# Query rows summed from PSUM, a second key pair in plain products, and a pair's last two products issued inside the next pair

## The chip, the cores and the metric

The kernel runs on one core of a Trainium2 chip. The metric is the device time of one execution in microseconds, from start to end, as the median of several runs. The core has a matrix engine (TensorE, in the profile PE, with its weight loads as PEld), a vector engine (VectorE, DVE), a scalar engine (ScalarE, ACT), GpSimd (POOL), and SyncE (SP), on whose queue this kernel issues its DMAs. TensorE writes only to PSUM, which has eight banks here; one product of 128x512 float32 fills one bank. All other tiles lie in SBUF.

## The reference, cut to what matters

There are 8 batch entries b of 128 rows x 512. Two layers run one after the other; the change concerns the first part of the first one, a gated cross attention with 32 heads of 128.

```python
x = rmsnorm(layernorm(hidden)) * ln_weight          # 8 x 128 x 512
h_q = (x @ w_q.T).reshape(b, 128, 32, 128)
h_k = (ctx @ w_k.T).reshape(b, 128, 32, 128)
h_v = (ctx @ w_v.T).reshape(b, 128, 32, 128)
score = softmax(where(mask, einsum('bqhd,bkhd->bhqk', h_q, h_k) + position_bias, -inf))
attn = einsum('bhqk,bkhd->bqhd', score, h_v)
out = hidden + attn.reshape(b, 128, 4096) @ w_out.T
```

Behind it come a dense layer with 4-bit weights, a second cross attention with a single head, and a dense layer with routed low-rank corrections; each is added to x through a gate tanh(g). All is float32.

## The kernel before, in words

**Products in three parts.** A float32 operand is split into a high part, rounded to the type that TensorE multiplies fast, and a low part, the rest (`split`, L162: the high by ACT at L163, the low by DVE or POOL at L164). A product is then three matmuls per 128 of the inner dimension: high x high, high x low, low x high (`product`, L166, lines 172 to 174).

**Seven products for eight.** Keys, queries and values are made by blocks of 2x2 with Winograd's scheme (`seven`, L219). A pair is two heads (2 x 128 output rows) by 512 inner by 1024 tokens. The left side (the weights) needs seven sums P1 to P7 (`left_parts`, L198), the right side (the transposed rows of all batch entries) seven blocks B11, B21, B22 and T1 to T4. Each of the seven products is six matmuls of 128x512. They are issued in the order P1, P5, P6, P2, P7, P4, P3 and add up in three PSUM banks: c1 takes P1, P6, P7 and P4, c3 takes P5 and P3, c2 takes P2. Between its uses c1 is read by copies of ACT: L251 after P1, L258 after P6, L267 after P7, L273 after P4. Sums on DVE follow (L262 after P2, L268 after P7, L277 after P3). So P7 has to wait for the copy of P6, P4 for the copy of P7, and P3 for the sum at L268. The four results of a pair lie in "kq" slots and go to DRAM (L493).

**The first pair** of keys is made plainly, in eight products of six matmuls, from the weights' rows split as they are and from the blocks B11, B12, B21, B22 of the context (`project_plainly`, L497), with two banks of "mm" and two of "av"; ACT copies them out at L517.

**The right sides.** `context_operands` (L429) splits the context's B blocks first (ACT high; POOL and DVE low), and then forms T1 to T4 on DVE (L451) and splits these. `query_operands` (L455) makes the rows of a pair of batch entries j and j+4 ready: `normed` (statistics and scaling on DVE, L416 to L422, a root on POOL, a scaling on ACT, L423), eight transposes on TensorE into two "av" banks, two copies to SBUF on ACT (L466), and then `right_parts` (L184): four sums on DVE and seven splits, lows on POOL. It is called after pairs 2, 5, 8 and 11 and does all of one j in one go.

**The order.** 32 pairs are made in this order: 14 of keys, 16 of queries, 2 of keys (L801). Pair n+2's weights are loaded and pair n+1's sums are formed while pair n is multiplied. Between them stand the steps of `early` (L715): 26 steps that load later weights, split them (ACT high, POOL low, some DVE) and store them to DRAM, one step after each pair from pair 3 on, save 5, 8 and 11; and `residual` (L531).

**The stages behind.** `unit(u)` (L867) runs 64 times: two output products of an earlier unit (`project_out`, "pso", in "mm" banks, evicted by DVE at L678), steps of the value products (`seven` with 256 columns, c1 in "mm", c3 in "av", c2 in "sc"), `attend` (L647, an "av" bank, read by ACT at L660 and DVE at L661) and `scores` (L596, an "sc" bank). The probabilities go through DRAM to be transposed by blocks (`move_probs`, L627, and L644). The rest of the layers runs at the end in `pipeline`, whose order on TensorE is kept as written.

**Slots, banks and planning.** Tiles with the same tag share a number of slots (`TAGS`) or banks (`BANKS`: 4 "mm", 2 "sc", 2 "av"); a new tile waits until the one that had its slot is read for the last time. When the kernel is built, a planner decides the order of the instructions on each engine with times of its own: of what is ready it takes what stands first in the program. So the program's order is a priority and not the order itself, except in `pipeline`. Each engine then runs its list strictly in order.

## Time and profile before

| | us |
|---|---|
| median of 3 runs | 1005.44 (1001.28 to 1006.37) |
| the profiled execution | 1005.73 |
| its span, first to last instruction | 1004.0 |
| TensorE (PE) busy | 937.9 (93%) |
| weight loads (PEld) busy | 808.1 (80%) |
| VectorE (DVE) busy | 664.1 (66%) |
| ScalarE (ACT) busy | 513.1 (51%) |
| GpSimd (POOL) busy | 495.5 (49%) |
| mean granted clock of TensorE | 0.983 |

Roughly, the projections of keys and queries fill the first 350 us, the units of attention the stretch to 860 us, and the later layers the rest. Busy time of TensorE overlaps from matmul to matmul: a matmul of 128x512 is listed with about 0.39 us, and the next one starts 0.23 us after it. So what a matmul costs in a row of them is the distance of the starts. "Waits" are idle times of an engine, put down to what ended them. A tile's name stands without its number (c_k is any of the banks c1, c2, c3 of a key pair).

### The profile page before, as it was taken

What the parts mean: (1) busy time and instruction counts of PE and PEld (TensorE: products, weight loads), DVE (VectorE), ACT (ScalarE), POOL (GpSimd) and SP (SyncE); (2) the same over time, 40 slices, a digit from 0 to 9 for tenths busy, and PEclk for the clock granted to TensorE, in tenths of its full rate; (3) what the DMA queues carried; (4) which work ended last, traced back from release to release, by engine and by line L of the source; (5) the groups of instructions that cost most, each with busy time, mean ns of one, the idle gap of its engine ahead of it and who ended that gap; (6) DMA issues with size and microseconds to landing.
All of it is one profiled execution on the core that took longest, in us unless ns stands there. A gap on an engine that the chain in (4) does not pass through costs nothing. (4 is left out here: it accounts for less than half of the span.)

```text
span 1004.0 us, 16700 instructions
## 1 busy us (share of the span) xinstructions
PE 937.9 (93%) x5438; PEld 808.1 (80%) x5438; DVE 664.1 (66%) x1335; ACT 513.1 (51%) x1444; POOL 495.5 (49%) x542
## 2 busy tenths in 40 slices
PE   6799999998999998999999999899999999899998
PEld 4568776776888798889989879788898898778897
DVE  7886576899666424666766576466765667645586
ACT  5566565754544544544434435244452453575762
POOL 4755355444000464683946638456486762462431
PEclk9899999999999999999999999899999999999999
DMA  8356567996545558765666766547565566613001
GB/s 284 110 168 207 161 192 247 321 313 201 182 149 162 156 160 246 226 186 170 184 184 157 200 165 176 182 128 205 169 176 182 166 180 199 220 43 129 1 22 64
DMA packets 125270, 175.01 MB, mean 174 GB/s; under 512 B 17406, under 2 KB 55294, under 8 KB 124030
## 3 DMA queue, kind: packets, MB, share of 16 engines
q1 hardware_dynamic: 125182, 173.94, 57.3%
q8 instruction: 43, 0.70, 0.3%
q14 instruction: 45, 0.37, 0.1%
HBM read 109.85 MB, written 64.03 MB: 173 GB/s over the span
## 5 line engine op out<-in xcount | busy, mean ns | idle before, releaser
L615 ACT ACTIVATE s<-s,nm 128x128 f32<-128x128 f32 x256 | 99.8, 391 | 166.8 <-DVE nm L608 98.1
L591 POOL TENSOR_TENSOR s<-mneg,bias 128x512 f32<-128x512 f32 x64 | 82.9, 1297 | 97.9 <-DMA through<-s 86.1
L644 DVE STREAM_TRANSPOSE pT<-moved 128x512 f32<-128x512 f32 x64 | 45.4, 710 | 98.5 <-DMA moved<-through 98.2
L164 POOL TENSOR_TENSOR wvP<-raw_wv,wvP 128x512 fp32r<-128x512 f32 x45 | 57.5, 1293 | 105.4 <-ACT wvP L163 105.4
L172 PE MATMUL pso<-wo_h,a 128*128 128x512 f32 x256 | 108.2, 423 | 0.4 <-ACT a L660 0.4
L174 PE MATMUL pso<-wo_h,a 128*128 128x512 f32 x256 | 102.6, 403 | 2.0 <-DVE a L661 2.0
L173 PE MATMUL pso<-wo_l,a 128*128 128x512 f32 x256 | 102.4, 400 | 0.0
L678 DVE SCALAR_TENSOR_TENSOR x<-pso,tg,x 128x512 f32<-128x512 f32 x128 | 93.3, 735 | 7.9 <-PE pso L174 7.8
L622 POOL TENSOR_TENSOR s<-s,rs 128x512 f32<-128x512 f32 x64 | 66.5, 1039 | 60.8 <-ACT wo_h L163 18.9
L172 PE MATMUL c_v<-wvP,cxT 128*128 128x256 f32 x288 | 83.1, 289 | 1.5 <-ACT v L267 0.7
L173 PE MATMUL c_v<-wvP,cxT 128*128 128x256 f32 x288 | 81.9, 284 | 0.0
L174 PE MATMUL c_v<-wvP,cxT 128*128 128x256 f32 x288 | 81.6, 284 | 0.0
L659 PE MATMUL av<-pT,v 128*128 128x128 f32 x512 | 69.9, 279 | 12.4 <-DVE a L661 11.5
L659 PEld LDWEIGHTS av<-pT,v 128*128 128x128 f32 x512 | 64.7, 193 | 17.7 <-issue 9.7
L603 PE MATMUL sc<-k,q 128*128 128x128 f32 x512 | 71.6, 280 | 4.3 <-DVE s L604 3.6
L603 PEld LDWEIGHTS sc<-k,q 128*128 128x128 f32 x512 | 66.6, 195 | 7.7 <-DVE s L604 4.5
L172 PE MATMUL c_v<-wvP,cxB 128*128 128x256 f32 x216 | 62.4, 289 | 5.0 <-DVE s L604 2.1
L173 PE MATMUL c_v<-wvP,cxB 128*128 128x256 f32 x216 | 61.4, 284 | 0.0
L174 PE MATMUL c_v<-wvP,cxB 128*128 128x256 f32 x216 | 60.9, 284 | 0.0
L172 PE MATMUL c_k<-cxT,wkP 128*128 128x512 f32 x120 | 49.3, 411 | 12.0 <-ACT keys L267 7.8
L172 PEld LDWEIGHTS c_v<-wvP,cxT 128*128 128x128 f32 x288 | 55.5, 193 | 5.2 <-ACT v L267 2.0
L174 PEld LDWEIGHTS pso<-wo_h,a 128*128 128x128 f32 x256 | 48.6, 190 | 13.4 <-DVE a L661 2.8
(270 smaller groups left out, 2811.6 us busy)
## 6 DMA issues: line engine op xcount, KB each, us to landing
keys<-keys SPq DMA_DIRECT2D x64, 256.0 KB, 3.5
queries<-queries SPq DMA_DIRECT2D x64, 256.0 KB, 2.9
q<-queries SPq DMA_DIRECT2D x64, 256.0 KB, 4.0
k<-keys SPq DMA_DIRECT2D x64, 256.0 KB, 4.7
through<-s SPq DMA_DIRECT2D x64, 256.0 KB, 2.6
moved<-through SPq DMA_DIRECT2D x256, 64.0 KB, 2.7
raw_wk<-in_wk_dram SPq DMA_DIRECT2D x32, 256.0 KB, 3.3
raw_wq<-in_wq_dram SPq DMA_DIRECT2D x32, 256.0 KB, 3.9
```

Of the source, the lines that this page charges most:

```text
L164: mark("low", (low_engine or nc.vector).tensor_tensor(low, src, wide(high), ALU.subtract))
L172: nc.tensor.matmul(out, lhsT=lh, rhs=rh, start=first, stop=False, **more)
L173: nc.tensor.matmul(out, lhsT=lh, rhs=rl, start=False, stop=False, **more)
L174: nc.tensor.matmul(out, lhsT=ll, rhs=rh, start=False, stop=last, **more)
L591: nc.gpsimd.tensor_tensor(s, mneg[:, half], bias.unsqueeze(2).to_broadcast([P, NQ, HALF, Q32]), ALU.add)
L603: nc.tensor.matmul(ps[:, j, :], lhsT=q[:, cols], rhs=k[:, cols], start=True, stop=True)
L615: e = nc.scalar.activation(one, one, AF.Exp, bias=nm[:, j : j + 1], accum_out=sm[:, j : j + 1])
L622: nc.gpsimd.tensor_tensor(s, s, rs.unsqueeze(1).unsqueeze(3).to_broadcast([P, NQ, HALF, Q32]), ALU.mult)
L644: nc.vector.transpose(by_block(t), probs[u])
L659: nc.tensor.matmul(av[:, b, :], lhsT=v[:, cols], rhs=pT[:, b, :], start=True, stop=True)
L678: "x", nc.vector.scalar_tensor_tensor(xs[b], ps, factor, xs[b], ALU.mult, ALU.add, **out)
```

## The change

The banks become 3 "mm", 2 "sc" and 3 "av". Pairs 0 and 1 of the keys are both made plainly, and the T blocks of the context are formed after the first of them. The seven sums of pair 2 have the lows of P1, P2 and P4 on POOL, as those of the pairs behind it had and have.

`query_operands` no longer copies the transposed rows to SBUF. The transposed blocks b11, b21 (one bank) and b12, b22 (the other) are read where they are: ACT copies b11 and takes the highs of B11, B21 and B22 from PSUM, DVE takes their lows and forms T1, T2 and T4 with one input in PSUM each; POOL forms T3 from SBUF. It comes in three pieces per j, one after each of the pairs 2 to 13: the first as above, the second T3 and the splits of T1 and T2, the third the splits of T3 and T4.

`project` now returns its steps, and the loop takes them so: P1 of the pair, P4 of the pair before, P5, P3 of the pair before, P6, P2, P7. The steps of `early` begin after pair 13, two after each pair.

```diff
--- before.py
+++ after.py
@@ -30,7 +30,7 @@
 RANK = 16
 MASKED = 1e30
 
-BANKS = {"mm": 4, "sc": 2, "av": 2}
+BANKS = {"mm": 3, "sc": 2, "av": 3}
 TAGS = {
     "page": 14, "v": 15, "wo": 8, "raw": 6, "kq": 6, "s": 3, "moved": 2, "pT": 2, "bias": 2,
     "pr": 4, "sel": 4,
@@ -181,20 +181,6 @@
     HK = NDC // 2
     N = HK * P
 
-    def right_parts(b11, b12, b21, b22, put):
-
-        put("B11", b11)
-        nc.vector.tensor_tensor(b11, b12, b11, ALU.subtract)
-        put("T1", b11)
-        nc.vector.tensor_tensor(b11, b22, b11, ALU.subtract)
-        put("T2", b11)
-        put("B21", b21)
-        nc.vector.tensor_tensor(b12, b22, b12, ALU.subtract)
-        put("T3", b12)
-        nc.vector.tensor_tensor(b21, b21, b11, ALU.subtract)
-        put("T4", b21)
-        put("B22", b22)
-
     def left_parts(a11, a12, a21, a22, more, engine, put):
 
         put("P1", a11)
@@ -454,6 +440,8 @@
 
     def query_operands():
 
+
+
         ops = right_pages("xq")
         for j in range(HALF):
             rows = [normed(j), normed(j + HALF)]
@@ -462,17 +450,31 @@
                 tp = ptile([P, NDC, P], "av", f"tpx_{j}_{half}")
                 for dc in range(NDC):
                     nc.tensor.transpose(tp[:, dc, :], rows[half][:, bass.ts(dc, P)], ident)
-                t = slot([P, NDC, P], "wo", f"xt_{j}_{half}")
-                nc.scalar.copy(t, tp)
-                blocks.append(t)
-            e, f = blocks
+                blocks += [tp[:, :HK], tp[:, HK:]]
+            b11, b21, b12, b22 = blocks
             cols = bass.ts(j, P)
 
-            def put(n, src):
+            def put(n, src, low=nc.gpsimd):
                 o = ops[n]
-                split(o[:, 0, :, cols], o[:, 1, :, cols], src, nc.gpsimd)
-
-            right_parts(e[:, :HK], f[:, :HK], e[:, HK:], f[:, HK:], put)
+                split(o[:, 0, :, cols], o[:, 1, :, cols], src, low)
+
+            def block(name):
+                return slot([P, HK, P], "wo", f"x{name}_{j}")
+
+            first, t1, t2, t3, t4 = (block(n) for n in ("B11", "T1", "T2", "T3", "T4"))
+            nc.scalar.copy(first, b11)
+            for n, src in (("B11", b11), ("B21", b21), ("B22", b22)):
+                put(n, src, nc.vector)
+            nc.vector.tensor_tensor(t1, b12, first, ALU.subtract)
+            nc.vector.tensor_tensor(t2, b22, t1, ALU.subtract)
+            nc.vector.tensor_tensor(t4, b21, t2, ALU.subtract)
+            yield
+            nc.gpsimd.tensor_tensor(t3, t2, first, ALU.subtract)
+            put("T1", t1)
+            put("T2", t2)
+            yield
+            put("T3", t3)
+            put("T4", t4)
             yield ops
 
     stored = {
@@ -492,7 +494,7 @@
         def done(i, half, t):
             nc.sync.dma_start(out=stored[kind, p][:, 2 * i + half], in_=t)
 
-        run(seven(f"{kind[0]}{p}", left, right, kept, done))
+        return seven(f"{kind[0]}{p}", left, right, kept, done)
 
     def project_plainly(kind, p, left, right):
 
@@ -797,44 +799,60 @@
         yield
 
 
+    BY_POOL = ("P1", "P2", "P4")
     BEFORE = NP - 2
     order = [("keys", p) for p in range(BEFORE)] + [("queries", p) for p in range(NP)]
     order += [("keys", p) for p in range(BEFORE, NP)]
-    first = []
-    for h in range(2):
-        high, low = (wide_row("v", f"wk_{n}{h}", F32R) for n in "hl")
-        split(high, low, raws.pop(f"wk_{h}"))
-        first.append((high, low))
+    def whole_pair(p):
+
+        both = []
+        for h in range(2 * p, 2 * p + 2):
+            high, low = (wide_row("v", f"wk_{n}{h}", F32R) for n in "hl")
+            split(high, low, raws.pop(f"wk_{h}"))
+            both.append((high, low))
+        return both
+
+    PLAIN = 2
+    left = whole_pair(0)
     making = context_operands()
     of_context = next(making)
-    project_plainly("keys", 0, first, of_context)
-    next(making)
     of_rows = query_operands()
     extra = early()
-    left = pair_parts("wk", 1)
+    before = iter(())
     for n, (kind, p) in enumerate(order):
-        if n == 0:
-            load_pair("wk", 2)
-            continue
         if n + 2 < len(order):
             k, q = order[n + 2]
             load_pair("w" + k[0], q)
+        if n < PLAIN:
+            project_plainly(kind, p, left, of_context)
+            left = whole_pair(p + 1) if p + 1 < PLAIN else pair_parts("wk", p + 1, BY_POOL)
+            if n == 0:
+                next(making)
+            continue
         following = None
         if n + 1 < len(order):
             k, q = order[n + 1]
-            following = pair_parts("w" + k[0], q, ("P1", "P2", "P4") if n < BEFORE else ())
-        project(kind, p, left, of_context if kind == "keys" else right)
+            following = pair_parts("w" + k[0], q, BY_POOL if n < BEFORE else ())
+        steps = project(kind, p, left, of_context if kind == "keys" else right)
         left = following
+
+        for _ in range(2):
+            next(steps)
+            next(before, None)
+        for _ in range(3):
+            next(steps)
+        before = steps
         if n == 3:
             prep_mask()
-        if n in (2, 5, 8, 11):
+        if n < BEFORE:
             right = next(of_rows)
         if n in (14, 16, 18, 20):
             residual((n - 14) // 2)
-        if n > 2 and n not in (5, 8, 11):
+        if n >= BEFORE - 1:
             next(extra, None)
-    for _ in extra:
-        pass
+            next(extra, None)
+    run(before)
+    run(extra)
     load_quad(0)
     run(quad_parts(0))
     for u in range(2):
```

## The prediction

> **What bounds the kernel now.** I read the stretches first, to see where TensorE is not full. Their columns are the stretch, then busy us and instructions of PE, PEld, DVE, ACT and POOL, then the granted clock, DMA share and GB/s.

> ```profile
> core 0: us, PE busy (x) PEld busy (x) DVE busy (x) ACT busy (x) POOL busy (x), PEclk, DMA share, GB/s
> 0.00:50.00 50.00, 33.37 (x117) 23.67 (x118) 39.13 (x79) 26.26 (x55) 28.73 (x46) 0.93 0.62 198
> 50.00:150.00 100.00, 93.53 (x399) 74.24 (x400) 71.83 (x128) 62.99 (x150) 46.54 (x55) 0.97 0.60 182
> 150.00:250.00 100.00, 92.27 (x387) 71.60 (x386) 85.12 (x164) 59.23 (x144) 50.09 (x45) 0.98 0.85 272
> 250.00:345.00 95.00, 93.98 (x416) 76.16 (x415) 59.52 (x134) 46.83 (x109) 4.03 (x4) 1.00 0.53 164
> ...
> 400.00:850.00 450.00, 430.36 (x2903) 392.01 (x2903) 294.99 (x529) 201.58 (x678) 275.95 (x232) 0.99 0.63 180
> 850.00:1004.00 154.00, 143.42 (x893) 123.97 (x891) 96.36 (x275) 91.15 (x246) 58.37 (x138) 0.99 0.23 81
> ```

> TensorE is the bound everywhere; all that can be won is its idle time and its time at half clock. It idles 16.6 us in the first 50, then 6.5, 7.7 and 1.0 in the three stretches of the projections, 19.6 between 400 and 850, and 10.6 in the tail. Between 250 and 345 it is full: in that stretch a pair's 42 products take 9.6 us, 0.23 us each, so there the order of the products loses nothing already. The waits of TensorE up to 345 us, total us, times, longest:

> ```profile
> PE c_k L172 <- ACT keys L267: 7.8, 4, 2.2
> ...
> PE c_k L174 <- DVE wkP L164: 5.0, 2, 4.3
> PE c_k L172 <- ACT keys L517: 3.1, 1, 3.1
> ...
> PE c_k L172 <- ACT keys L251: 1.2, 2, 0.8
> ```

> Two places hold most of it. The first is the change from the plain pair to the first pair of seven, in the timeline of PE (start, duration, what ended the wait):

> ```profile
> 25.62 0.50 PE L172 MATMUL c_k<-cxT,wkP 128*128 128x512 f32 x1 [3.11 <-ACT keys L517]
> ...
> 29.03 0.50 PE L172 MATMUL c_k<-cxT,wkP 128*128 128x512 f32 x1 [0.85 <-ACT keys L251]
> ...
> 34.11 0.80 PE L174 MATMUL c_k<-cxT,wkP 128*128 128x512 f32 x1 [4.34 <-DVE wkP L164]
> ```

> After the 4.34 us the products start 0.43 us apart instead of 0.23 for 3.4 us: a long wait is followed by a stretch at half clock, which costs another 1.7 us. The second place recurs each time a pair of rows becomes query operands. Here is the one at 102.6 us:

> ```profile
> 99.71 1.23 DVE L422 SCALAR_TENSOR_TENSOR xq<-x,stats,lnw 128x512 f32<-128x512 f32 x1
> ...
> 101.74 1.22 DVE L422 SCALAR_TENSOR_TENSOR xq<-x,stats,lnw 128x512 f32<-128x512 f32 x1
> ...
> 102.99 0.72 ACT L423 ACTIVATE xq<-xq,stats 128x512 f32<-128x512 f32 x1 [0.30 <-DVE xq L422]
> ...
> 104.62 0.57 ACT L267 COPY keys<-c_k 128x512 f32<-128x512 f32 x1
> ...
> 105.25 0.50 PE L172 MATMUL c_k<-cxT,wkP 128*128 128x512 f32 x1 [2.25 <-ACT keys L267]
> ```

> TensorE waits for a copy that stands in ScalarE's queue behind the rows' work, and that waits for VectorE. VectorE is late because operations with both inputs in SBUF take twice their time beside POOL, while those that read PSUM do not. Duration min/median/max in ns:

> ```profile
> L189 DVE TENSOR_TENSOR xt<-xt,xt x4: 957/957/1510, 67.4 to 165.2; 128x256 f32<-128x256 f32 x4
> ...
> L262 DVE TENSOR_TENSOR keys<-c_k,keys x13: 675/690/693, 41.0 to 177.0; 128x512 f32<-128x512 f32 x13
> ```

> In the attention stage the longest wait of TensorE is for the one "av" bank that the open value product leaves free:

> ```profile
> PE av L659 <- DVE a L661: 11.5, 11, 2.5
> ```

> **The change, part by part.** The sum is made against the profiled execution, 1005.7 us (span 1004.0 and 1.7 around it), 0.3 above the median of the three runs, 1005.44.

> *The second pair in eight products.* A plain pair has 48 products of 128x512, a pair of seven 42: 6 more by 0.2275 us is +1.4, on the path. It moves the first use of the T operands and of the seven sums of a pair back by the plain pair's 48 x 0.2275 = 10.9 us. The last low half of T was done at 32.3 us (POOL, cxT, 30.98 + 1.33), and pair 1's plain products would end at about 21 + 11 = 32. So the waits at 25.62, 27.45, 29.03, 34.11 and 41.00 (3.11 + 0.17 + 0.85 + 4.34 + 0.67 = 9.1) with the half clock behind them (1.7) can go: 10.8 at most, 0 at least. What is late next: the copies out of the first pair's banks (ran at 24.0, ready to start before 21), of which the second pair needs two within 3 us, and T itself, now just in time. I take three quarters, -8.1. The plain pair 1 needs two rows split (each 0.62 on ACT and 0.69 on DVE) in place of seven parts; its rows are loaded second on SP's queue and issued by 7.9 us, and no load moves past another on SP that is wanted earlier.

> *Row sums from PSUM, in three pieces.* Per pair of rows ACT loses two copies (0.58 each) and gains one of half the size (0.41 at most): -0.75. POOL loses three lows and gains one sum: 7 x 0.8 to 5 x 0.8, -1.6. DVE goes from four sums to three sums and three lows, all with one input in PSUM. No row shows such an operation at 128x256: it costs between 0.41 (L187's shortest) and 0.96 (L189's median), so six are 2.5 to 5.8 us against about 3.3 now. L262, L268 and L277 stay within 671 and 693 ns whatever POOL does, so I take 0.42, 2.5 us. The two "av" banks of the transposes are now held until the sums are done, some 3 us; with the open c3 that is all three, and the next pair's P5 waits for one, but P1, P4, P3, P6 and P2 stand ready, 30 products or 6.8 us, so I cost it at nothing. Moved with it: the early weights' 26 steps start at pair 13 instead of pair 3, two per pair. The eight items whose lows (1.36 each on POOL) and copies (0.62 on ACT) lay beside the rows leave that place, with their loads and stores on SP. All together this bears on the four waits for L267 (7.8) and three half-clock stretches after them at 106, 140 and 174 us (5.1): 12.9 at most. But L422 with its two SBUF inputs stays, with L423 behind it, and they stood right ahead of the late copy in the lines above; below, rows can also get worse (a rival). I take half, -6.5.

> *A pair's last products between the next one's.* The planner already does it: at 258.65 us, right behind P7, it issues the next pair's P1, and then P4. Nothing is to be won where ACT is in time; after it P6 to P7 have one product (1.4 us) between them instead of two, with a copy of 0.59 to hide: nothing lost either. I cost it at 0, and the cover is that 1.4 us; an ACT that is over 0.8 us late shows there.

> *The banks, 3/2/3 for 4/2/2.* In the attention stage the value product holds one "mm" and one "av" bank nearly all the time. I compared in the trace each group's first product with the end of the evacuation that it would have to wait for. For attend's bank the wait is real now: 11.5 us, and a half-clock stretch after the one at 561 us (1.7). With a second bank all 62 starts have at least 0.5 us to spare: -13.2. For the output products (pso) three banks gave one conflict; with two, 14 of 126 starts come before the eviction (L678) two groups back has ended, by 27.3 us summed. 18.2 of these are three groups at 411 to 424 us, of one backlog of DVE, which overlap (one wait of 7.4 covers the next), and the other eleven are 9.1, the largest 3.75. Between 0 and 27.3, then; I take 10 (the other eleven and a little of the first, since the planner places them knowing the banks). Net -3.2. In the tail the evictions three groups back are over before each start in the trace's order: 0.

> Sum: -8.1 + 1.4 - 6.5 - 3.2 = -16.4, 1005.7 to 989.3.

> **The rivals.**

> *The lost "mm" bank decides (slower).* VectorE's backlogs (it waits 98 us for the moved probabilities) now stop TensorE at pso, twice in a unit, and what attend no longer waits for is only waited for elsewhere: 27.3 lost and nothing of the 13.2 won, 1005.7 - 8.1 + 1.4 - 6.5 + 27.3 = 1019.8. For it speaks that pso's margin falls from a median of 5.9 us to 1.9. Against it, attend's rises from 2.1 to 9.4. It decides against the change once pso's waits pass the 26.4 that the rest wins.

> *Row blocks in PSUM tie ACT to DVE.* The copies by ACT and the lows by DVE now read the same bank; if they are kept apart, ACT's next high waits until DVE's low is done, with all that stands before it in DVE's queue, and the copies of c1 behind it. Then the four waits double instead of halving: +12.9 for -6.5, 1008.7. No row of before has both engines on one bank without a dependency of data. [...]

> *The early weights crowd the queries.* From 150 to 250 us, with 85% of DVE busy, TensorE lost 7.7 idle and 2 by the clock. With two items a pair that loss doubles and lasts 13 pairs, 125 us: 24.3 instead of 9.7, 1003.9. For it: DVE was 47.5 of 50 us busy from 200 on. Against: the items were held by slots, not by their place in the order, and ran in bursts already.

> *All goes.* Every wait named vanishes and pso never waits: -10.8 - 12.9 - 13.2 + 1.4, 970.2.

> **How the numbers follow.** The forecast with its sizes half out, 980 to 1000, has 0.50; all or nearly all goes (980 and below) 0.15; the early weights 0.10; the tied engines 0.08; the lost bank 0.17. I predict 989, with a range of 970 to 1012, which leaves out the lost bank and a little below 970. Under half a per cent, about 5 us here, is what this kernel's runs can't tell from no change. Faster takes the first two, 0.65; same the next two, 0.18; slower the last, 0.17.

> **What would show it.** In the profile after: no wait over 1 us of TensorE between 21 and 35 us, and 96 products before the first T operand; the waits for L267 at most half of 7.8 with the rows' sums at about 0.42 us each; no wait for L661 at L659; waits of pso's first product (L172) for L678 of about 10 us; the pairs from 250 us still 9.6 us each; early items from about 140 us on. Wrong it would be if pso's waits come to 25 us, if ACT's casts of xqB wait for DVE, or if the first pair of seven still stalls for T.

## The result and the profile after

The changed kernel takes 975.05 us (median) beside 1003.36 us for the kernel before, run with it: a ratio of 0.9715, with a 95% interval of 0.9676 to 0.9755. Run a second time from the same source on another chip, with the same order of instructions on TensorE, VectorE, ScalarE and GpSimd (after_again below), it took 978.32 beside 1002.18, a ratio of 0.9751 (0.9714 to 0.9787). So it is faster by about 24 to 28 us. The forecast was 989, that is 16 us faster; the time lies inside the range of 970 to 1012, and the gain is bigger than forecast: 975 and 978 belong to the case "all or nearly all goes", which had a chance of 0.15, and not to the one that had 0.50.

The profiled execution took 976.61 us (span 974.8), 1.6 above the median; the one of before took 1005.73. First the stretches of the changed kernel, with the columns of those shown before: busy us and instructions of PE, PEld, DVE, ACT and POOL, then granted clock, DMA share and GB/s. All work comes earlier than before, so that the same stretch holds somewhat later work.

```profile
core 0: us, PE busy (x) PEld busy (x) DVE busy (x) ACT busy (x) POOL busy (x), PEclk, DMA share, GB/s
0.00:50.00 50.00, 38.91 (x153) 29.65 (x154) 39.44 (x78) 29.42 (x63) 32.32 (x49) 0.97 0.68 219
50.00:150.00 100.00, 94.53 (x412) 75.94 (x411) 69.72 (x136) 58.77 (x145) 35.86 (x45) 0.98 0.50 152
150.00:250.00 100.00, 92.96 (x404) 74.91 (x403) 89.35 (x167) 60.55 (x147) 45.09 (x40) 1.00 0.92 303
250.00:345.00 95.00, 90.38 (x405) 74.18 (x404) 60.20 (x122) 46.01 (x104) 19.21 (x15) 1.00 0.53 169
...
400.00:850.00 450.00, 438.01 (x2952) 396.83 (x2951) 307.25 (x552) 207.15 (x682) 280.70 (x250) 1.00 0.63 186
```

In the first 50 us TensorE issues 153 matmuls instead of 117, in the next stretch 412 instead of 399. Between 250 and 345 it is less full than it was (90.38 busy, was 93.98): two waits for the copy behind P7, 3.9 together, fall there, and the first group of experiments shows why. Between 400 and 850 its idle time falls from 19.6 to 12.0 us.

The waits of TensorE up to 325 us (total us, times, longest). L253 is the copy of c1 behind P7 that was L267 before.

```profile
PE c_q L172 <- ACT queries L253: 8.1, 6, 2.4
...
PE c_k L172 <- ACT keys L253: 4.9, 7, 2.5
PE c_k L174 <- DVE wkP L164: 2.2, 2, 1.7
PE c_k L174 <- POOL wkP L164: 1.4, 1, 1.4
PE tpx L452 <- ACT keys L519: 1.2, 2, 1.0
```

The change from plain pairs to pairs of seven, which had waits of 3.11 and 4.34 us and a half-clock stretch behind them, has no wait over 1.4 (the one of 1.7 is at 53.6 us). The wait for the copy behind P7 is not gone: for keys it is 4.9 where it was 7.8, but for queries it is 8.1 where it was 2.8 (9.7 and 3.5 with the queries that come after these windows). Only three half-clock stretches are left in this execution, at 40.4, 139.4 and 849.4 us, where there were eight; after_again has four.

From 325 to 860 us, in the attention stage (L661 is attend's product of probabilities and values, L646 the transpose of the probabilities to pT, L680 the eviction of pso):

```profile
PE av L661 <- DVE pT L646: 4.2, 6, 1.1
PE pso L172 <- DVE x L680: 3.6, 8, 0.9
```

No wait for attend's bank (L663) at L661 is left, of 11.5 us before. In its place attend's product waits 4.2 for its probabilities, and pso waits 3.6 for its bank.

**Time lost by stage.** Where the gain came from is read best from the starts of the matmuls. In an unbroken row of these profiles they stand 0.2275 us apart with 512 columns, 0.119 with 256, 0.121 with 264 and 0.111 with 128. The time from one matmul to another less the sum of these distances is lost time, whether idle or at half clock. The first three columns go by the count of the matmuls of keys and queries; "to scores" ends with the first scores product, and "units" runs from there to the last one.

| kernel | 1 to 144 | 144 to 700 | 700 to 1200 | to scores | units |
|---|---|---|---|---|---|
| before | 19.2 | 16.8 | 7.4 | 3.3 | 39.7 |
| after | 10.1 | 10.9 | 10.4 | 3.2 | 22.2 |
| after_again | 10.2 | 9.3 | 10.4 | 3.9 | 24.0 |
| b_plain2 | 10.4 | 17.4 | 8.3 | 1.5 | 38.4 |
| b_plain2_late | 10.0 | 12.1 | 8.8 | 1.6 | 36.8 |
| a_422_turn | 11.8 | 4.2 | 8.9 | 1.6 | 37.0 |
| a_banks422 | 10.7 | 4.3 | 8.4 | 0.4 | 29.5 |
| a_in_turn | 10.1 | 19.4 | 22.9 | 5.7 | 28.3 |
| b_banks323 | 17.2 | 37.5 | 17.0 | 5.7 | 36.7 |
| b_banks322 | 19.0 | 31.7 | 15.9 | 2.8 | 37.3 |
| a_early | 10.1 | 16.1 | 9.5 | 2.9 | 23.3 |
| a_rows_sbuf | 10.5 | 9.8 | 5.1 | 2.8 | 22.8 |
| a_c3_mm | 11.2 | 4.4 | 7.6 | 0.1 | 26.4 |
| a_best2 | 10.7 | 3.9 | 3.1 | 0.1 | 26.6 |

From before to after: -9.1 - 5.9 + 3.0 - 0.1 - 17.5 = -29.6, and +1.4 for the six products more is -28.2, of -29.2 in the spans. Of the 17.5 in the units, 6.8 is half clock: in the kernel before, 13.7 us of that stage passed at half clock, in the changed kernel none. The other 11 are idle time, 22.1 before and 10.8 after. Each row is one execution; the two executions of the changed kernel (after and after_again) differ by up to 1.8 in a column. Names with b_ are the kernel before with a part of the change, names with a_ the changed kernel with a part undone or altered.

### The profile page after: what moved, and what is told of

Its sections match the earlier page's. It is cut to its first block, busy times and chain, and to the rows that moved or that the text cites. A ratio compares the mean times of both kernels' runs of the same rounds, so it can differ in the third digit from the quotient of the medians.

```text
span 974.8 us, 16753 instructions
## 1 busy us (share of the span) xinstructions
PE 926.3 (95%) x5444; PEld 803.9 (82%) x5444; DVE 668.1 (69%) x1331; ACT 504.7 (52%) x1435; POOL 489.0 (50%) x534
## 5 line engine op out<-in xcount | busy, mean ns | idle before, releaser
L172 PE MATMUL pso<-wo_h,a 128*128 128x512 f32 x256 | 107.9, 422 | 3.8 <-DVE x L680 3.6
L646 DVE STREAM_TRANSPOSE pT<-moved 128x512 f32<-128x512 f32 x64 | 45.4, 709 | 86.8 <-DMA moved<-through 86.2
L174 PE MATMUL pso<-wo_h,a 128*128 128x512 f32 x256 | 101.7, 398 | 2.0 <-DVE a L663 2.0
L680 DVE SCALAR_TENSOR_TENSOR x<-pso,tg,x 128x512 f32<-128x512 f32 x128 | 93.4, 738 | 7.9 <-PE pso L174 7.9
L164 POOL TENSOR_TENSOR wvP<-raw_wv,wvP 128x512 fp32r<-128x512 f32 x45 | 57.7, 1296 | 70.9 <-ACT wvP L163 70.9
L172 PE MATMUL c_v<-wvP,cxT 128*128 128x256 f32 x288 | 82.3, 286 | 0.7 <-ACT v L253 0.7
L174 PE MATMUL c_v<-wvP,cxT 128*128 128x256 f32 x288 | 81.3, 283 | 0.0
L661 PE MATMUL av<-pT,v 128*128 128x128 f32 x512 | 68.6, 276 | 5.2 <-DVE pT L646 4.2
L661 PEld LDWEIGHTS av<-pT,v 128*128 128x128 f32 x512 | 64.4, 192 | 9.4 <-issue 2.7
L605 PE MATMUL sc<-k,q 128*128 128x128 f32 x512 | 69.1, 276 | 1.9 <-issue 1.3
L605 PEld LDWEIGHTS sc<-k,q 128*128 128x128 f32 x512 | 63.4, 192 | 3.6 <-issue 1.7
L172 PE MATMUL c_v<-wvP,cxB 128*128 128x256 f32 x216 | 61.7, 286 | 1.6 <-DVE v L254 1.4
L174 PE MATMUL c_v<-wvP,cxB 128*128 128x256 f32 x216 | 61.1, 283 | 0.0
L172 PE MATMUL c_q<-xqT,wqP 128*128 128x512 f32 x128 | 50.9, 397 | 10.1 <-ACT queries L253 9.7
L174 PEld LDWEIGHTS pso<-wo_h,a 128*128 128x128 f32 x256 | 48.6, 190 | 13.9 <-DVE a L663 2.8
L164 POOL TENSOR_TENSOR wkP<-raw_wk,wkP 128x256 fp32r<-128x256 f32 x36 | 28.5, 795 | 62.8 <-ACT wkP L163 57.7
```

What stands on the lines that cost most here:

```text
L164: mark("low", (low_engine or nc.vector).tensor_tensor(low, src, wide(high), ALU.subtract))
L172: nc.tensor.matmul(out, lhsT=lh, rhs=rh, start=first, stop=False, **more)
L174: nc.tensor.matmul(out, lhsT=ll, rhs=rh, start=False, stop=last, **more)
L605: nc.tensor.matmul(ps[:, j, :], lhsT=q[:, cols], rhs=k[:, cols], start=True, stop=True)
L646: nc.vector.transpose(by_block(t), probs[u])
L661: nc.tensor.matmul(av[:, b, :], lhsT=v[:, cols], rhs=pT[:, b, :], start=True, stop=True)
```

## The experiments

My theory after the result was that of the prediction with larger sizes: waits at the head, late rows and the one attend bank had each given way, and the order did nothing. The rival was that the parts are not separate: that three "mm" banks cost much in the projections, and that the new order is what pays for them.

### The order and the banks

The five kernels of this group differ from the kernel before (b_) or the changed one (a_) in two things, the banks and whether the products of a pair are issued in one go.

a_in_turn is the changed kernel with the loop's order undone:

```diff
-        for _ in range(2):
-            next(steps)
-            next(before, None)
-        for _ in range(3):
-            next(steps)
-        before = steps
+        run(steps)
```

> The changed kernel with each pair's seven products in one go again, in the program's order P1, P5, P6, P2, P7, P4, P3, nothing else changed. My step costs this part at 0, since the planner puts the next pair's P1 behind P7 by itself: 973 to 978 us, and the waits for the copy of P7 stay at about 13 us. Rival (written into the order it does carry part of the projections' gain): 980 to 987 us, lost before 350 us.

Measured: 1010.89 us, 1.0054 (1.0023 to 1.0086): the whole gain of the change is gone, though all its other parts are there. The theory's 973 to 978 is far off, and the rival had the place right but not the size. (The profiled execution took 1005.85; the ten lie between 1001 and 1014.) The waits up to 345 us:

```profile
PE c_q L172 <- ACT queries L253: 13.8, 14, 3.7
PE c_k L172 <- ACT keys L253: 9.0, 8, 3.1
```

The timeline of a_in_turn at 296 us, where neither rows nor early weights disturb, first PE's last matmul of P7, then ACT's copy, then PE's first matmul of P4:

```profile
296.14 0.39 PE L174 MATMUL c_q<-xqT,wqP 128*128 128x512 f32 x1
...
296.57 0.59 ACT L253 COPY queries<-c_q 128x512 f32<-128x512 f32 x1 [0.95 <-PE c_q L174]
...
297.21 0.50 PE L172 MATMUL c_q<-xqT,wqP 128*128 128x512 f32 x1 [0.68 <-ACT queries L253]
```

Here P4 follows P7 directly, with nothing between them to hide the copy: the starts are 1.07 us apart instead of 0.23. From 264 to 360 us this comes once in each pair; the copy of the pair before is at 286.08 us, 10.49 us earlier. In the changed kernel another product goes on in that gap:

```profile
296.67 0.59 ACT L253 COPY queries<-c_q 128x512 f32<-128x512 f32 x1 [0.86 <-PE c_q L174]
...
296.70 0.39 PE L173 MATMUL c_q<-xqT,wqP 128*128 128x512 f32 x1
296.93 0.39 PE L174 MATMUL c_q<-xqT,wqP 128*128 128x512 f32 x1
```

and its copy before that is at 287.15, so that a pair takes 9.52 us. For 30 pairs of seven the difference of 0.97 comes to an estimated 29 us; by the table the columns from 144 to the scores lose 23.5 more than in the changed kernel.

Which product stands in the gap can be read from its operand: P1, P2 and P3 read a B block (xqB), P5, P6, P7 and P4 a T block (xqT). In the kernel before it reads a B block, and by the count below it is a P1:

```profile
258.43 0.39 PE L174 MATMUL c_q<-xqT,wqP 128*128 128x512 f32 x1
...
258.65 0.39 PE L172 MATMUL c_q<-xqB,wqP 128*128 128x512 f32 x1
...
258.85 0.59 ACT L267 COPY queries<-c_q 128x512 f32<-128x512 f32 x1 [0.86 <-PE c_q L174]
```

In the changed kernel's lines above it reads xqT, and is a P5: ACT's copies behind P6, P7 and P4 show where these three stand.

Counting the products shows whose they are. When the P7 of pair k (k from 0, of the pairs of seven) is copied, the pairs so far need 3k+2 products with a B block and 4k+3 with a T block. Away from the rows 3k+6 and 4k+5 have been issued in a_in_turn, 3k+6 and 4k+4 in the kernel before and in the changed one. So P1 and P2 of the next two pairs are done by then, and P5 of the next two pairs in a_in_turn, of the next one in the other two.

A pair holds an "mm" bank from its P1 until P4 is copied, an "sc" bank for P2 and an "av" bank from P5 to the sum behind P3. In a_in_turn three pairs then hold three "mm", two "sc" and three "av" banks, all eight. P4 alone can set one free, and it waits for the copy. P6 of the next pair needs no new bank, but the copy of its P1 stands behind the copy of P4 in ACT's queue. So nothing can start. In the same place the kernel before has its fourth "mm" bank left, and P1 of the third pair ahead goes into it. The changed kernel has its third "av" bank left, and P5 of the second pair ahead goes into that; the written order leaves this P5 for the gap.

The same count works pair by pair, when the "av" banks that the transposed rows hold are added and the last two pairs left out. In the changed kernel all eight banks are held at 14 of 28 copies behind P7; TensorE waits at these 14 and at no other. In a_in_turn it waits at 24 of 27 such copies, in b_banks323 and b_banks322 below at 28 of 28.

b_banks323 is the kernel before with the new banks and nothing else:

```diff
-BANKS = {"mm": 4, "sc": 2, "av": 2}
+BANKS = {"mm": 3, "sc": 2, "av": 3}
```

> The kernel before with only the banks changed to 3 mm, 2 sc, 3 av. Theory (the banks alone make the attention stage faster): from the first scores product to the last one 463 us before becomes about 450, as after the change; TensorE's waits for the sum at L661 go from 11.5 us to under 1, the stretches at half clock in that stage go, pso waits for L678 stay under 5 us; the projections stay as they are; 988 to 993 us in all. Rival (the stage is faster for another reason, the new plan or what is handed over to it by the projections): the stage stays within 4 us of 463 and the whole within 4 us of 1003.

Measured: 1027.99 us, 1.0249 (1.0203 to 1.0295), slower by 24 or 25 us, where the theory had a gain and the rival no change. The loss lies in the projections (37.5 instead of 16.8 in one column, 17.0 instead of 7.4 in the next) and not at pso. Its waits up to 345 us, and then those from 345 to 860:

```profile
PE c_k L172 <- ACT keys L267: 16.4, 12, 4.6
PE c_q L172 <- ACT queries L267: 12.4, 12, 2.5
...
PE av L659 <- DVE pT L644: 12.2, 10, 2.8
PE pso L172 <- DVE x L678: 3.8, 8, 1.1
```

The waits for L267, 7.8 for keys and 2.8 for queries in the kernel before, come to 28.8; pso's are 3.8.

b_banks322 takes the "mm" bank away and gives it to no one (`"mm": 3, "sc": 2, "av": 2`).

> The kernel before with one mm bank less and nothing in its place (3 mm, 2 sc, 2 av). It measures the price of the lost mm bank by itself. My prediction put it at 10 us, between 0 and 27. Theory (the planner places the output products with the banks in mind, so the loss is small): 1003 to 1008 us. Rival (the lost bank costs its 10 us or more, and the third av bank wins more than that): 1013 us or more, with pso waiting for L678 10 us or more.

Measured: 1027.17 us, 1.026 (1.0202 to 1.0319). Without the third "av" bank the loss is the same, so it is the missing "mm" bank's alone: 14.9 and 8.5 us more lost than before in the two columns of the projections. The units lose 2.4 less than before. The rival had the time, but not the reason: pso waits 4.1 us for L678 and not 10.

a_banks422 is the changed kernel with the old banks (`"mm": 4, "sc": 2, "av": 2`).

> The changed kernel with the old banks (4 mm, 2 sc, 2 av). Theory of the banks: the attention stage goes back to about 463 us with some 10 us of waits for the sum on DVE behind attend, and the projections lose a few us where the open c3 and the two transposes want three av banks: 988 to 995 us. Rival (the banks matter little): 975 to 980 us.

Measured: 976.41 us, 0.9745 (0.9707 to 0.9784): no different from the changed kernel. The projections lose 11 us less (4.3 + 8.4 + 0.4 against 10.9 + 10.4 + 3.2), and the units 7.3 more, with the wait for attend's bank back. Its waits for the copy behind P7 up to 345 us, and the one for attend's bank from 345 to 860:

```profile
PE c_k L172 <- ACT keys L253: 2.6, 2, 1.3
PE c_q L172 <- ACT queries L253: 2.3, 2, 1.8
...
PE av L661 <- DVE a L663: 4.5, 4, 1.7
```

a_422_turn has both undone, the old banks and the seven products in one go.

> The changed kernel with the old banks (4 mm, 2 sc, 2 av) and each pair's seven products in one go: the fourth case of banks and order in the changed kernel, beside 975 (new banks, interleaved), 976 (old banks, interleaved) and 1011 (new banks, in one go). Theory (the third av bank was paid for with the mm bank by which the planner put the next pair's P1 ahead of P4, and the written order only gives that back): 976 to 984 us, with the late pairs 9.6 us apart and no wait for the copy of P7 in them. Rival (the written order helps with any banks): 990 to 1011 us.

Measured: 981.72 us, 0.9783 (0.9746 to 0.9821). So with four "mm" banks the written order is worth 0.4% (3.8 us, inside the intervals) and nothing at all in the projections (4.2 and 8.9 lost, with it 4.3 and 8.4). With three it is worth 30 to 36 us. What three banks still cost is in the waits for L253 over all pairs: 4.9 + 9.7 us in the changed kernel, 2.6 + 2.3 with four. With three "mm" banks one P5 stands in that place, 1.4 us long; with four, in a_banks422 at 287.2 us, a P1 and a P5 do, 2.7 us. Where ACT is late and the P5 has been used up before, TensorE stops for up to 2.4 us (at 246.7 and 259.6 us in the changed kernel). The four corners, in us: 975 to 978 with new banks and new order, 976 with old banks and new order, 982 with both old, 1011 with new banks and old order.

What follows: the new order is there to make three "mm" banks bearable, and the third "av" bank about pays for what three "mm" banks still cost. Together the two are worth 3 to 7 us against both old, at the edge of what the runs tell apart. That P1 is missing from the gap with three banks follows from the banks held, as counted above; why the planner runs P1, P2 and P5 that far ahead was not looked into.

after_again is the changed kernel unaltered, as a measure of scatter.

> The changed kernel as it is, for a second profile and beside the others on one chip. 972 to 978 us. The time that TensorE loses between the first and the last scores product was 22.2 us in its first profile; within 4 us of that the differences of that stage between the kernels (22 to 40 us) stand, beyond it they are scatter.

Measured: 978.32 us, 0.9751 (0.9714 to 0.9787). The instructions come in the same order as in the first profile, so the difference of 3 us is one of chips and executions. Steps of 3 or 4 us between kernels are at the edge of what these runs tell apart.

### The second plain pair and the early steps

b_plain2 is the kernel before with the second plain pair alone (T is formed after the first pair, and the lows of P1, P2 and P4 of the next pair are on POOL, as in the change):

```diff
+        if n < 2:
+            project_plainly(kind, p, left, of_context)
+            left = whole_pair(1) if n == 0 else pair_parts("wk", 2, ("P1", "P2", "P4"))
+            if n == 0:
+                next(making)
+            continue
```

> The kernel before with only the second key pair made plainly (and T formed after the first pair), banks and order as before. Theory (this part wins by itself what my first term said): the time that TensorE loses up to its 144th product goes from about 19 us to about 10, less 1.4 for the six more products; 994 to 999 us, as all the kernels with two plain pairs so far lost 10 us there and all those with one 17 to 19. Rival (it is given back in the next pairs, whose operands are then late): 1001 to 1005 us.

Measured: 993.71 us, 0.9929 (0.9902 to 0.9956), 7.1 us faster. The first column falls from 19.2 to 10.4, and no other changes by more than 1.8.

b_plain2_late adds the later start of the early steps:

```diff
-        if n > 2 and n not in (5, 8, 11):
+        if n >= BEFORE - 1:
             next(extra, None)
+            next(extra, None)
```

> The kernel before with two plain pairs (the run b_plain2, 993.7) and the early weights' steps after pair 13, two after each, as after the change; rows summed in SBUF in one go, order and banks as before. The run a_422_turn (981.7) is this kernel with the rows' sums in PSUM. Theory (the late steps alone win the 12 us between b_plain2 and a_422_turn; the sums in PSUM cost about 4): 976 to 981 us, and TensorE loses about 4 us between products 144 and 700. Rival (both are needed, since beside POOL's lows only the sums in PSUM are not slowed): 985 to 992 us.

Measured: 989.13 us, 0.9849 (0.9815 to 0.9883), 8.0 us below b_plain2. Of it 5.3 lie where the rows are made ready (17.4 to 12.1 lost); behind, where two steps a pair now fall, the loss is 8.8 against 8.3.

a_early is the test from the other side, the changed kernel with the early steps at their old place, one a pair from pair 3 on:

```diff
-        if n >= BEFORE - 1:
-            next(extra, None)
+        if n > 2 and n not in (5, 8, 11):
             next(extra, None)
```

> The changed kernel with the early weights' steps back at their old places, one after each pair from 3 on but 5, 8 and 11. Theory (beside the rows they cost POOL's and DVE's time, and later they crowd the queries): 3 to 6 us more lost between products 144 and 700, 2 or 3 us less between 700 and 1200; 975 to 980 us. Rival (slots hold them wherever they stand in the program): within 2 us of 975.

Measured: 981.77 us, 0.9816 (0.9779 to 0.9853): slower than the two executions of the changed kernel by 6 and 10 us in the ratios, 3 and 7 in the medians, with 16.1 lost instead of 10.9 (9.3) where the rows are made. Both tests agree on the place and, in lost time, on the size: 5 to 7 us.

### The rows' sums

a_422_turn, shown above, is b_plain2_late with the sums from PSUM in three pieces: 0.9849 to 0.9783, some 6.6 us, and 12.1 to 4.2 lost in the column of the rows. a_rows_sbuf is the changed kernel with only this part undone: the transposed rows copied to SBUF, summed there and split in one go after pairs 2, 5, 8 and 11.

```diff
-                blocks += [tp[:, :HK], tp[:, HK:]]
+                t = slot([P, NDC, P], "wo", f"xt_{j}_{half}")
+                nc.scalar.copy(t, tp)
+                blocks.append(t)
...
+            right_parts(e[:, :HK], f[:, :HK], e[:, HK:], f[:, HK:], put)
...
-        if n < BEFORE:
+        if n in (2, 5, 8, 11):
             right = next(of_rows)
```

> The changed kernel with the rows copied to SBUF, summed there and split in one go after pairs 2, 5, 8 and 11, as before; early steps, order and banks as after the change. Theory (the rows' part is worth its term of 6.5 us): TensorE loses 16 to 20 us between products 144 and 700 instead of 10.9; 980 to 986 us. Rival (the order carries the whole gain there, the place of the sums nothing): 973 to 978 us.

Measured: 971.52 us, 0.9696 (0.9665 to 0.9726): not slower, by its ratio 2 to 5 us faster. The sums themselves behave as the prediction said. In the changed kernel (duration min/median/max in ns, first and last start) two of the sums from PSUM, and the scaling L408 that still reads SBUF twice:

```profile
L468 DVE TENSOR_TENSOR xT<-tpx,xB x4: 414/415/416, 45.4 to 151.1; 128x256 f32<-128x256 f32 x4
...
L469 DVE TENSOR_TENSOR xT<-tpx,xT x4: 409/424/425, 47.9 to 151.6; 128x256 f32<-128x256 f32 x4
...
L408 DVE SCALAR_TENSOR_TENSOR xq<-x,stats,lnw x8: 715/1060/1683, 28.4 to 118.1; 128x512 f32<-128x512 f32 x8
```

and in a_rows_sbuf two of the sums with both inputs in SBUF (busy us, mean ns of one):

```profile
L446 DVE TENSOR_TENSOR xt<-xt,xt 128x256 f32<-128x256 f32 x4 | 3.6, 912 | 0.0
...
L444 DVE TENSOR_TENSOR xt<-xt,xt 128x256 f32<-128x256 f32 x4 | 2.3, 563 | 0.0
```

Sums from PSUM take 0.41 to 0.43 us; from SBUF these two take 0.41 to 0.96. The place of the inputs alone does not decide it. In a_rows_sbuf 136 sums of this size, of rows and of weights, have both inputs in SBUF: 88 of them meet no instruction of POOL and take 0.41 to 0.43, the 48 that meet one take up to 1.52. The sums and lows from PSUM in the changed kernel take 0.43 at most, 14 of them beside POOL.

But under the new order the lateness that the slow sums from SBUF cause no longer stops TensorE more than the sums from PSUM do: 9.8 lost in the rows' column against 10.9 and 9.3. With four "mm" banks the four cases are clearest: in the old order the column loses 12.1 with sums in SBUF (b_plain2_late) and 4.2 from PSUM (a_422_turn), in the new order 3.9 (a_best2, below) and 4.3 (a_banks422). The two parts cover the same wait, and the second one to come is worth nothing. With three "mm" banks sums from PSUM even have a price: a bank of transposed rows is held 1.2 to 6.5 us in a_rows_sbuf, until it is copied; in the changed kernel the first one of each two, whose b21 is read last, is held 12.6 to 17 us, and meanwhile there is one "av" bank less for a P5. The wait of 2.48 at 138.55 us falls there (held from 135.41 to 152.46). The column from 700 to 1200, where queries are multiplied, loses 5.1 us with sums in SBUF and 10.4 with sums from PSUM; why was not looked into. Nor were the place of the sums and their three pieces tried one without the other.

### Two versions beyond the change

If the third "av" bank is worth 5 us in the units and the fourth "mm" bank 11 in the projections, a kernel should have both. In the units the value product's c3 holds one of the "av" banks. a_c3_mm keeps the old banks and puts c3 of the value products alone ("tokens" is given only there) into "mm":

```diff
-BANKS = {"mm": 3, "sc": 2, "av": 3}
+BANKS = {"mm": 4, "sc": 2, "av": 2}
...
-        c3 = ptile(shape, "av", f"c3_{name}")
+        c3 = ptile(shape, "av" if tokens is None else "mm", f"c3_{name}")
```

> The changed kernel with the banks of before (4 mm, 2 sc, 2 av) and the value products' c3 in an mm bank instead of an av bank, so that the projections have 4 and 2 banks as in the run a_banks422, and attend has two banks for itself as after the change. Theory (four mm banks are worth 9 us in the projections under the new order, a second bank for attend is worth 7 us in the attention stage): 965 to 970 us. Rival (the difference of the attention stages was not the banks, as the run b_banks323 suggests, which had them and lost as much there as before): 973 to 978 us.

Measured: 966.55 us, 0.9629 (0.9587 to 0.9672), 10 to 12 us below a_banks422 and 9 to 12 below the changed kernel. It loses 4.4, 7.6 and 0.1 in the projections, like a_banks422, and 26.4 in the units, near the changed kernel's 22.2 and 24.0.

a_best2 adds to it the rows in SBUF of a_rows_sbuf (its diff and the one above together).

> The run a_c3_mm (966.5) with the rows copied to SBUF and summed in one go after pairs 2, 5, 8 and 11, as before. Theory (the row sums from PSUM cost more than they win, as the run a_rows_sbuf suggests by 3.5 us): 961 to 965 us. Rival (that difference was scatter between plans): 965 to 970 us.

Measured: 962.82 us, 0.9611 (0.9572 to 0.9651), the fastest median of this study, 10 to 15 us under the changed kernel and 39 under the one before. Its step below a_c3_mm lies inside the intervals, so that by the times alone the rival stands; but the column from 700 to 1200 falls by 4.5, as it did by 5 or so from the changed kernel to a_rows_sbuf. Its stretches between 50 and 345 us:

```profile
50.00:150.00 100.00, 98.15 (x442) 80.04 (x441) 74.89 (x141) 66.88 (x162) 45.16 (x56) 1.00 0.54 168
150.00:250.00 100.00, 97.55 (x426) 79.29 (x425) 93.46 (x176) 62.05 (x150) 49.39 (x42) 1.00 0.90 310
250.00:345.00 95.00, 94.29 (x460) 79.55 (x460) 54.33 (x112) 48.18 (x105) 27.48 (x22) 1.00 0.55 175
```

TensorE idles 5 us in these 295, where the changed kernel idles 17.

## Why the prediction was right and where it was wrong

**The second plain pair: right.** Forecast -8.1 + 1.4 = -6.7, measured -7.1. Of the waits of 9.1 with the half clock behind them, 4.0 of waits are left in the changed kernel between 33.8 and 40.5 us (the largest 1.36, for a low of the weights), and one half-clock stretch at 40.4; in b_plain2 it is one wait of 3.7 for a high of the weights. Three quarters was about the right share. The cover that I named held: 102 matmuls, not 54, now stand ahead of the first with a T operand, and none waits for T; the sign "no wait over 1 us of TensorE between 21 and 35 us" is missed by one wait of 1.02. What is late next is mostly the weights' parts (2.9 of the 4.0); the copies that I had named take 1.2, and T nothing.

**Rows and early steps: the mechanism right, the term too small.** I took half of 12.9, -6.5. Measured from b_plain2 to a_422_turn it is 0.9929 to 0.9783, -14.6, and in the trace 17.4 to 4.2 lost in the rows' column, -13.2: the whole of the 12.9. The reason that I gave for half was that L422 with its two SBUF inputs stays slow. It does (L408 above, 0.72 us at the shortest, median 1.06, up to 1.68; all eight meet an instruction of POOL), but no longer stops TensorE: in a_422_turn no product of keys waits for the copy behind P7. The mark I had set for this, waits for L267 at most half of 7.8, would have misled: in the changed kernel the keys' waits are 4.9, because the banks add to the same line, and 2.6 where the banks are the old ones (a_banks422). More than half of the term by the ratios (8.0 of 14.6) is the early steps' and not the rows'; I had put both into one sum. In the lost time the rows have the larger share (7.9 of 13.2), so the split is open by some 3 us; the sum is not. One part I put at nothing with a wrong size: the "av" banks of the transposes, which I took to be held some 3 us, are held up to 17, and under the new order that costs the P5 its place.

**The order at 0: right for four banks, wrong for this change.** "The planner already does it" was read at 258.65 us in the trace of before, and with four "mm" banks it is true (a_422_turn against a_banks422). But that P1, by the count the one of the third pair ahead and not "the next pair's", stood there in a fourth bank, which the same change takes away. The order is worth 30 to 36 us of the changed kernel's time. The mark I had set, pairs 9.6 us apart from 250 on, shows it: 9.52 with the order, 10.49 without. What covers the copy of P7 now is a P5 in the third "av" bank. My cover for the edit, "P6 to P7 have one product between them", was looked for in the wrong place: the one that counts is between P7 and P4.

**The banks at -3.2: near the net, for the wrong reasons.** Both terms were mis-sized, and one was missing. Attend's bank: I took -13.2. Between kernels with the same order, the units lose 5.3 less with two banks for attend (means 37.8 and 32.5 in the old order, 29.5 and 24.2 in the new one; the single profiles scatter by as much). The wait for the bank is gone as forecast, but part of it comes back as the wait for pT (4.2 us, and 12.2 in b_banks323): I had looked only at the bank and not at what arrives next. pso: I took +10, measured 3.6 (8 waits, none over 0.9). Missing was the projections' price of the "mm" bank: +23 in the old order (b_banks322), +11 in the new one (a_banks422 to after). I had compared starts with evacuations for pso and attend alone. The net of banks in the new order is +0.6 or -3.0 us, by the two executions; that it lies near -3.2 is luck.

**The units.** They lost 39.7 and now lose 22.2, -17.5, where I forecast -3.2. The bank accounts for about 5 and the order for about 8 (means 37.8 to 29.5 with one bank and 32.5 to 24.2 with two). Part of that is half clock: in lost time it is 5.1 us of a_422_turn's units, 3.4 of a_banks422's and b_banks323's, none of a_in_turn's, and whether a wait brings it is in part chance, as the last section shows. What the order of the projections changes there besides was not looked into further, and the ratios give the order no more than 3.8 with old banks, so this part is argued from single profiles.

**The rivals.** "The lost bank decides" was forecast at 1019.8 with its price at pso. It is not what happened here, but b_banks323, at 1028, is that case, with the price elsewhere: I had the danger and not the place. "Row blocks in PSUM tie ACT to DVE": no run shows that the two engines have to be kept apart on a bank, on which the 12.9 I allowed rests. In the changed kernel's trace no read of the transposed blocks by ACT overlaps one by DVE, and ACT's casts of xqB wait for DVE once, 0.2 us. "Early weights crowd the queries": the column from 700 to 1200 rises by 3.0 and not by 14.6, and a_rows_sbuf and a_best2, with late steps too, have 5.1 and 3.1, less than the 7.4 of before; late steps gain overall (8.0 us from b_plain2 to b_plain2_late). "All goes", 970.2, was closer to the result than my forecast, by the rows' term.

**The sum.** In profiled executions -29.1 against -16.4: rows and early steps 8 more than forecast, the other 5 between the order (-3.8 by the ratios, forecast 0) and scatter. The banks came out near their net by the errors in it that cancelled.

## What to carry to other kernels

When a trace shows that the planner already does what an edit writes out, ask which banks or slots it does it with, and whether the same change takes them away. Count the products issued up to the wait: they tell how many banks are held and which product could still start. A bank moved between tags has a price in every stage that uses the tag: look for it in each of them, and try whether a tile can change its tag in one stage alone, as c3 did for about 10 us. Two edits that cover the same wait are not summed; undo each in the presence of the other to see which one is still needed.

## What the runs showed of the hardware

A half-clock stretch came behind waits shorter than itself. This is TensorE in the changed kernel at 138.55 us, with the matmuls behind it:

```profile
138.55 0.50 PE L172 MATMUL c_k<-cxT,wkP 128*128 128x512 f32 x1 [2.48 <-ACT keys L253]
...
140.15 0.63 PE L174 MATMUL c_k<-cxT,wkP 128*128 128x512 f32 x1
140.58 0.63 PE L172 MATMUL c_k<-cxT,wkP 128*128 128x512 f32 x1
```

After a wait of 2.48 us the starts go 0.43 apart for 3.4 us, which costs 1.7 more; in the kernel before the stretch at 106 us followed the wait of 2.25. Behind the waits of 0.68 in a_in_turn, at 286.71 and 297.21 us, the starts are 0.23 apart from the second matmul on.

How long a wait is does not settle it alone. The same wait, 2.36 us for the copy of the same pair, leaves the clock alone in the changed kernel's first profile:

```profile
259.62 0.50 PE L172 MATMUL c_q<-xqT,wqP 128*128 128x512 f32 x1 [2.36 <-ACT queries L253]
259.95 0.39 PE L173 MATMUL c_q<-xqT,wqP 128*128 128x512 f32 x1
```

and sets it back in after_again:

```profile
256.72 0.80 PE L172 MATMUL c_q<-xqT,wqP 128*128 128x512 f32 x1 [2.36 <-ACT queries L253]
257.31 0.63 PE L173 MATMUL c_q<-xqT,wqP 128*128 128x512 f32 x1
```
